# A four-layer graph network on one core: layer 3's tiles multiplied in runs of four, with a buffer pool shared with layer 2's edge tiles

## The chip, the cores and the metric

The kernel runs on one core of a Trainium2 chip. The core has five engines that matter here: TensorE (PE in the profile; PEld is its weight load), VectorE (DVE), ScalarE (ACT), GpSimd (POOL) and SyncE (SP). Each works through its own list of instructions in order, and they wait for each other by semaphores. The time is device microseconds from the runs of the whole program; the figure that counts is their median.

## The reference

There are 16 graphs of 1024 nodes with 256 features, and a symmetric 0/1 edge matrix for each. Four layers follow one another, each on a normalized input, with the input added to its result:

```python
h = jnp.maximum(_layernorm(x, axis=-1), 0.0)
x = x + _L0_gnn_ref(h, adj, L0_gnn_W, L0_gnn_a)       # attention, softmax over axis 1
h = jnp.maximum(_layernorm(x, axis=-1), 0.0)
x = x + _L1_gnn_ref(h, adj, L1_gnn_W, L1_gnn_a)       # attention, softmax over axis 2
h = jnp.maximum(_layernorm(x, axis=-1), 0.0)
x = x + _L2_gnn_ref(h, adj, L2_gnn_W_msg, L2_gnn_W_upd, L2_gnn_bias)
h = jnp.maximum(_layernorm(x, axis=-1), 0.0)
x = x + _L3_gnn_ref(h, adj, L3_gnn_W, L3_gnn_a_src, ...)
```

Layer 2 is the mean over the neighbours, a product of the edge matrix with the projected features:

```python
a = adj.astype(x.dtype)
h = jnp.einsum('bnf,fu->bnu', x, W_msg)
msg_sum = jnp.einsum('bij,biu->bju', a, h)
deg = jnp.sum(a, axis=1)
messages = jnp.where(deg[..., None] > 0, msg_sum / jnp.maximum(deg, 1.0)[..., None], 0.0)
out = jnp.einsum('bnf,fu->bnu', x, W_upd) + messages + bias
```

Layer 3 is an attention with four heads of 64 features, then a normalization over each head:

```python
weight = weight + mask * (e_src[:, :, t, :, None] + e_dst[:, :, t, None, :])
weight = jax.nn.leaky_relu(weight, negative_slope=0.01)
weight = jnp.where(node_adj[:, None] == 0, NEG, weight)
attention = jax.nn.softmax(weight, axis=-1)
dst = jnp.einsum('bhij,bhje->bhie', attention, h) + bias[None, :, None, :]
out = jax.nn.relu(dst) + h
```

## The kernel before

The kernel has two versions of the work; for these inputs the one in `tile_simple_stack` runs, and everything below is in it. A tile is 128 rows of a graph's 1024, so a graph has eight (NT).

**The order of the work.** Each graph is a Python generator that gives out its instructions and yields how many microseconds it thinks they take. The loop at the end takes the generators by their clocks: a graph starts 120 planned microseconds after the one before it (APART), and its own plan is about 260 long, so two graphs are always interleaved. By that plan layer 3 of a graph lies beside layer 0's products and layer 1's beginning of the next graph, and layer 2 beside layer 0's projections. The order of giving out is a priority, not the final order: when the program is built, the instructions of each engine are ordered by when they are estimated to be ready. `later` (`tc.keep_in_program_order`) pins an instruction behind the one given out before it on the same engine. A tile with a tag takes one of the tag's `bufs` buffers; the instruction that first writes it waits until a buffer has been released by the last user of its former tile.

**Layer 2** (`layer2`, from L890) multiplies the edge matrix as weights: for each of eight column blocks j, one edge tile of 512 KB (`load_adj`, L584, a DMA from GpSimd's queue at L589) is used by L922 with the projected features, split in a high and a low part. The tag "adj" has four buffers. Four tiles are loaded at the layer's start, and each block's end gives out the load four blocks on.

**Layer 3** (`layer3`, from L939): for each head h and each tile j, VectorE makes an attention tile p of 128x1024 by L968 from a row that lies in all partitions, a column q and the mask, in one instruction. TensorE then multiplies it (L981) as weights with the 64 features of the head and a column of sums, in halves of 64 columns, into two PSUM banks that hold all eight output tiles. The tiles are taken in runs of two; all products of a run follow its last p, since the first product of the run reads that one. The last graph takes runs of one. The tag "p3" has five buffers; two weight tiles at the start and `sq` in `tail` use it too.

Beside it on the engines are layer 0's products (L790), the transposes of the normalization (L684), the projections (L690), and layer 1's tiles p1 (L861) and products (L854). The rows of the attention layers go through DRAM: `spread` writes them (L709), `everywhere` reads them back into all partitions (L715), both from SyncE's queue, which also loads the pieces of the transposed edge matrix for the masks (raw, L568). ScalarE turns these into the mask bytes (L581). GpSimd makes the powers for the normalizations (`inv_std`, L596 and L597), and its queue issues the edge loads and the loads of x (L547).

Of the kernel before, what the change touches and what calls it, by code (L numbers as in the profile page):

```python
# [14 lines left out]
P = 128  # L15
# [406 lines left out]
def tile_simple_stack(  # L422
# [24 lines left out]
    HW = HO + 1  # L447
    STEP = 1.48
    EARLY = 2

    const = ctx.enter_context(tc.tile_pool(name="const", bufs=1))
    dram = ctx.enter_context(tc.tile_pool(name="dram", bufs=2, space=bass.MemoryType.DRAM))
# [44 lines left out]
    def weights01(layer, w, w_t, a, order, wait=True):  # L497

        wx[layer] = t = load_w(w, D, f"wx{layer}", D + 2, wait)
        wts = work.tile([P, N], F32, tag="p3", name="wts", bufs=5)[:, : DC * D].rearrange("p (c f) -> p c f", c=DC)  # L500
        if wait:
            behind(wts[:1, 0, :1])
        later(nc.sync.dma_start(wts, w_t.rearrange("(c p) f -> p c f", p=P)))
        avs = small.tile([P, DC, 2], F32, tag="avs", name="avs", bufs=1)
        later(nc.sync.dma_start(avs, a.rearrange("(c p) k -> p c k", p=P)))
        for fc in range(DC):
            ps = mm_ps.tile([P, HALF], F32, tag="mm", name="ps_wa")
            for ec in range(DC):
                nc.tensor.matmul(
                    ps[:, :2], wts[:, ec, fc * P : (fc + 1) * P], avs[:, ec, :], start=(ec == 0), stop=(ec == DC - 1)  # L510
                )
            for k, to in enumerate(order):
                nc.vector.tensor_copy(t[:, fc, D + to : D + to + 1], ps[:, k : k + 1])
# [11 lines left out]
    def weights3():  # L525

        wx[3] = t = load_w(w3, D, "wx3", W3)
        w3ts = work.tile([P, N], F32, tag="p3", name="w3ts", bufs=5)[:HO, :].rearrange("p (h f) -> p h f", h=H)
# [54 lines left out]

    def load_adj(b, g):  # L584

        t = state.tile([P, NT, EIGHTH], F32R, tag="adj", name="adj", bufs=4)
        if b == 0 and g < 4:
            behind(t[:1, 0, :1])
        nc.gpsimd.dma_start(t, adj[b, :, g * EIGHTH : (g + 1) * EIGHTH].rearrange("(i p) c -> p i c", p=P))  # L589
        return t  # L590


# [236 lines left out]
    def layer1(b, xs, mask, norm, after):  # L829
# [23 lines left out]
        def product(ps, i, j):  # L853
            nc.tensor.matmul(  # L854
                ps[:, : D + 1], ps_[j][:, i * P : (i + 1) * P], hs[:, j, : D + 1], start=(j == 0), stop=(j == NT - 1)
            )
# [9 lines left out]
        for i in range(NT):  # L866
            if i < len(early):
                ps = early[i]
            else:
                ps = at_ps.tile([P, HALF], F32, tag="at", name="ps_o1")  # L870
                for j in range(NT):
                    product(ps, i, j)
            k = b * NT + i
            z = shares[:, k : k + 1]
            nc.vector.reciprocal(z, ps[:, D : D + 1])
            e = work.tile([P, D], F32, tag="e", name="e")
            nc.scalar.activation(e, ps[:, :D], AF.Exp, scale=z)
# [13 lines left out]
    def layer2(b, xs, norm, after):  # L891
# [2 lines left out]

        adj_n = [load_adj(b, g) for g in range(4)]
        z = small.tile([P, NT], F32, tag="z2", name="z2", bufs=2)
        nc.vector.reciprocal(z, norm.times)
        hi = state.tile([P, NT, W3], F32R, tag="hs", name="hi", bufs=3)  # L900
# [12 lines left out]
        for j in range(NT):  # L913
# [10 lines left out]
                        start=False, stop=(h is lo and i == NT - 1), skip_group_check=True,  # L924
                    )
            k = b * NT + j
            if j + 4 < NE:
                adj_n.append(load_adj(b, j + 4))
            v = work.tile([P, D], F32, tag="v", name="v")
            nc.scalar.activation(v, ps[:, :D], AF.Copy, scale=z[:, j : j + 1])  # L930
            nc.scalar.copy(edges[:, k : k + 1], ps[:, D : D + 1])
# [5 lines left out]
    def layer3(b, xs, mask, norm, res):  # L937
        hs = new_hs()
        terms = hs[:, :, D:]  # L939
        run = 2 if b < B - 1 else 1  # L940
        hb = new_hs("hb")
        hbv = hb[:, :, : H * HW].rearrange("p t (h e) -> p t h e", e=HW)
        for n in range(NT):
# [17 lines left out]
        for h in range(H):  # L961
            next_row = everywhere(d_row[h + 1], "row3") if h + 1 < H else None
            pss = [hd_ps.tile([P, HALF], F32, tag="hd", name="ps_o3") for _ in range(NHALF)]
            for j in range(0, NT, run):
                ps_ = []
                for jj in range(j, j + run):
                    p = work.tile([P, N], F32, tag="p3", name="p3", bufs=5)
                    nc.vector.scalar_tensor_tensor(p, row, q[:, jj, h : h + 1], mask[:, jj, :], op0=OP.max, op1=OP.mult)  # L968
                    ps_.append(p)


                last = run - 1
                runs = [(last, 0), (last, PER)] + [(t, i) for t in range(run) for i in range(NT) if t < last or i % PER]
# [3 lines left out]
                for t, i in runs:  # L977
                    g, k = divmod(i, PER)
                    for c in range(2):
# [3 lines left out]
                            start=(j == 0 and t == last and k == 0), stop=(j == NT - run and t == last and k == PER - 1),  # L983
                            skip_group_check=True,
                        )
                yield 1.4 * run
            for g in range(NHALF):
                o = pss[g][:, : PER * HW].rearrange("p (k e) -> p k e", e=HW)
                nc.scalar.activation(res[:, g * PER : (g + 1) * PER, h, :], o, AF.Relu)  # L989
# [3 lines left out]
    def tail(b, xs, hs, res):  # L993
# [4 lines left out]
        for g in range(NHALF):  # L998
# [15 lines left out]
            sq = work.tile([P, N], F32, tag="p3", name="sq", bufs=5).rearrange("p (k e) -> p k e", e=HO)  # L1014
            nc.scalar.activation(sq, o, AF.Square)
            halves.append((t, o, of, m, sq))
        rs = []
# [45 lines left out]
        hs = yield from layer3(b, xs, m.bytes, norm, res)  # L1063
        return tail(b, xs, hs, res)

    loaded, masks = {}, {}

    def loads(b):
        loaded[b] = load_x(b)
# [109 lines left out]
```

## Time and profile before

| what | value |
|---|---|
| median of three runs | 2609.52 us (2608.33 to 2610.64) |
| the profiled execution: its time, its span | 2612.95 us, 2611.1 us |
| mean granted TensorE clock | 0.987 |
| instructions | 63088 |
| edge loads (L589): number, size, median from issue to landing | 128, 512 KB, 4.8 us |
| moved by DMA in all | 232.17 MB, 89 GB/s on average |

The span is what the hardware profiler saw from the first to the last instruction; the run's time has a little around it. In the pages a group of instructions has its line, its engine, what it writes and reads, how often it ran, its busy time, the mean of one, and the idle time of the engine just before it with what ended that. In a timeline each row starts with the start and the length in us, and the idle time before it stands in brackets. Of the waits, those of GpSimd are the longest (it waits for ScalarE 1537.6 us and for L922 477.9 us), but it is busy for only 17% of the span.

### The profile page before, as it was taken

How to read it: one execution, taken by the hardware profiler on the slowest of the kernel's cores; microseconds unless marked ns; L12 is line 12 of the kernel's file. 1: busy time of each engine (PE TensorE's matmuls, PEld its weight loads, DVE VectorE, ACT ScalarE, POOL GpSimd, SP SyncE). 2: the span in 40 equal slices, each digit the busy share in tenths (PEclk: the TensorE clock that was granted, in tenths of full speed). 3: DMA queues.
4: the chain of work that ended last, by engine and by line, in shares of the span. 5: the costliest groups of instructions: out<-in, count | busy, mean ns of one | idle time of the engine just before them, and what ended most of it. 6: DMA issues, size and time to landing. Idle time of an engine off the chain costs nothing.

```text
span 2611.1 us, 63088 instructions
## 1 busy us (share of the span) xinstructions
PE 2462.2 (94%) x26224; PEld 2102.5 (81%) x26224; DVE 1978.2 (76%) x3862; ACT 1431.3 (55%) x4036; POOL 449.9 (17%) x454
## 2 busy tenths in 40 slices
PE   6999999999999999999999999999999999999975
PEld 4788887888888888887888878888887888878864
DVE  6458778687777878778687777878768697777858
ACT  3763755637475563755637465563755637465350
POOL 1020211203021120211203021120211203011021
PEclk8999999999999999999999999999999999999987
DMA  4541522625225151522615224261522515224021
GB/s 136 111 85 55 141 54 78 130 66 131 62 89 103 62 134 55 134 58 80 132 59 137 63 86 105 63 134 55 134 58 80 133 57 138 64 67 103 25 65 36
DMA packets 212152, 232.17 MB, mean 89 GB/s; under 512 B 10344, under 2 KB 160976, under 8 KB 211856
## 3 DMA queue, kind: packets, MB, share of 16 engines
q1 hardware_dynamic: 74128, 144.14, 17.6%
q0 software_dynamic: 137728, 83.90, 17.2%
q8 instruction: 208, 3.41, 0.5%
q14 instruction: 88, 0.72, 0.1%
HBM read 210.78 MB, written 17.22 MB: 87 GB/s over the span
## 4 chain that ended last, share of the span: by engine, by line
PE 57%; DVE 17%; DMA 11%; ACT 10%; issue 3%; POOL 2%; SPq 0%; DVEq 0%; POOLq 0%; ACTq 0%
PE ps_o L790 16%; PE ps_proj L690 12%; PE ps_o L981 10%; DVE p L968 6%; PE ps_o L922 6%; PE ps_o L854 5%; DMA row<-d_row 5%; PE pt_h L684 5%; DVE p L861 4%; DMA raw<-in_adj_t 4%; PE ps_o L916 3%; ACT mask L581 2%; DMA d_row<-e_row 2%; ACT hn L671 2%; ACT unread L644 2%
## 5 line engine op out<-in xcount | busy, mean ns | idle before, releaser
L968 DVE SCALAR_TENSOR_TENSOR p<-row,q,mask 128x1024 f32<-128x1024 f32 x512 | 632.3, 1280 | 66.9 <-PE ps_o L981 55.7
L981 PEld LDWEIGHTS ps_o<-hb,p 128*64 128x64 f32 x16384 | 505.4, 138 | 101.8 <-DVE p L968 40.3
L981 PE MATMUL ps_o<-hb,p 128*64 128x65 f32 x16384 | 541.7, 224 | 28.7 <-DVE p L968 18.6
L690 PE MATMUL ps_proj<-wx,ht 128*128 128x258 f32 (+2 forms) x2048 | 509.8, 388 | 3.5 <-ACT hs L770 2.3
L790 PE MATMUL ps_o<-hs,p 128*128 128x256 f32 x2048 | 493.3, 386 | 18.8 <-ACT hs L804 18.8
L854 PE MATMUL ps_o<-hs,p 128*128 128x257 f32 x2048 | 496.9, 389 | 8.6 <-DVE p L861 8.6
L790 PEld LDWEIGHTS ps_o<-hs,p 128*128 128x128 f32 x2048 | 379.5, 191 | 75.0 <-ACT hs L804 23.2
L690 PEld LDWEIGHTS ps_proj<-wx,ht 128*128 128x128 f32 x2048 | 366.2, 191 | 77.2 <-ACT hs L770 9.7
L854 PEld LDWEIGHTS ps_o<-hs,p 128*128 128x128 f32 x2048 | 375.3, 191 | 62.9 <-DVE p L861 10.3
L596 POOL TENSOR_SCALAR rs<-mv 128x4 f32<-128x4 f32 (+1 forms) x112 | 41.2, 367 | 1557.4 <-ACT unread L644 1537.6
L597 POOL TENSOR_TENSOR rs<-rs,neg_half 128x4 f32<-128x4 f32 (+2 forms) x144 | 261.7, 1818 | 11.8
L759 DVE SCALAR_TENSOR_TENSOR xs<-e,xs 128x256 f32<-128x256 f32 x256 | 108.0, 422 | 180.7 <-ACT e L822 133.4
L671 ACT ACTIVATE hn<-xs,shift 128x256 f32<-128x256 f32 x384 | 175.2, 502 | 124.9 <-DVE shift L639 118.3
L684 PE MATMUL pt_h<-ident,hn 128*128 128x128 f32 x1024 | 181.8, 289 | 42.8 <-ACT hn L671 41.8
L922 PE MATMUL ps_o<-hi,adj 128*128 128x258 f32 x1024 | 203.2, 321 | 1.6
L684 PEld LDWEIGHTS pt_h<-ident,hn 128*128 128x128 f32 x1024 | 115.7, 142 | 110.0 <-ACT hn L671 93.2
L589 POOL DMA_DIRECT2D adj<-in_adj x128 | 114.5, 895 | 479.5 <-PE ps_o L922 477.9
L581 ACT ACTIVATE mask<-raw 128x512 uint8<-128x512 int32 x240 | 150.1, 626 | 69.7 <-DMA raw<-in_adj_t 42.8
L760 DVE SCALAR_TENSOR_TENSOR xs<-v,xs 128x256 f32<-128x256 f32 x384 | 161.4, 423 | 29.4 <-ACT v L824 16.5
L800 DVE SCALAR_TENSOR_TENSOR p<-row,q 128x1024 f32<-128x1024 f32 x128 | 161.8, 1274 | 18.5 <-DMA row<-d_row 16.9
L989 ACT ACTIVATE res<-ps_o 128x260 f32<-128x260 f32 x128 | 46.4, 374 | 232.4 <-PE ps_o L981 232.1
L922 PEld LDWEIGHTS ps_o<-hi,adj 128*128 128x128 f32 x1024 | 152.5, 190 | 14.2 <-ACT hi L908 4.8
(115 smaller groups left out, 3035.9 us busy)
## 6 DMA issues: line engine op xcount, KB each, us to landing
raw<-in_adj_t SPq DMA_DIRECT2D x256, 256.0 KB
adj<-in_adj POOLq DMA_DIRECT2D x128, 512.0 KB, 4.8
row<-d_row SPq DMA_DIRECT2D x109, 512.0 KB
xs<-in_x POOLq DMA_DIRECT2D x32, 512.0 KB, 7.1
out<-xs SPq DMA_DIRECT2D x32, 512.0 KB
wx<-in_w SPq DMA_DIRECT2D x3, 256.0 KB
d_row<-e_row SPq DMA_DIRECT2D x45, 4.0 KB
wts<-in_w_t SPq DMA_DIRECT2D x2, 256.0 KB
```

Source lines behind the costliest of these rows:

```text
L581: nc.scalar.activation(to, raw, AF.Square, accum_out=total)
L597: nc.gpsimd.tensor_tensor(rs[:, :n], rs[:, :n], neg_half[:, :n], op=OP.pow)
L671: nc.scalar.activation(hn, xs[:, 2 * g + k, :], AF.Relu, scale=scale, bias=bias)
L684: nc.tensor.transpose(pt[:, c, k * P : (k + 1) * P], hn[:, c * P : (c + 1) * P], ident)
L690: nc.tensor.matmul(ps[:, :width], norm.ht[:, c, n * P : (n + 1) * P], w[:, c, :width], start=(c == 0), stop=(c == DC - 1))
L760: nc.vector.scalar_tensor_tensor(x, v, 0.0, x, op0=OP.max, op1=OP.add, accum_out=after.sums[:, i % 2 : i % 2 + 1])
L790: m = nc.tensor.matmul(ps[:, :D], ps_[j][:, i * P : (i + 1) * P], hs[:, j, :D], start=(j == 0), stop=(j == NT - 1))
L800: nc.vector.scalar_tensor_tensor(p, row_a, q[:, j : j + 1], row_b, op0=OP.mult, op1=OP.max)
L854: nc.tensor.matmul(ps[:, : D + 1], ps_[j][:, i * P : (i + 1) * P], hs[:, j, : D + 1], start=(j == 0), stop=(j == NT - 1))
L922: nc.tensor.matmul(ps[:, : D + 2], adj_n[j][:, i, :], h[:, i, : D + 2], start=False, stop=(h is lo and i == NT - 1), skip_group_check=True,)
L968: nc.vector.scalar_tensor_tensor(p, row, q[:, jj, h : h + 1], mask[:, jj, :], op0=OP.max, op1=OP.mult)
L981: nc.tensor.matmul(pss[g][part, k * HW : (k + 1) * HW], ps_[t][:, i * P : (i + 1) * P][:, part], hbv[:, j + t, h, :], start=(j == 0 and t ...
```

## The change

Three things are changed together. Layer 3 takes its tiles in runs of four (the last graph still in runs of one), and inside a run it yields once in the middle, so that the planned pace per tile is as before. The tag "adj" is gone: the edge tiles take the tag "p3", which now has nine buffers, as many as the two tags had together, in the same size. And the edge loads are given out elsewhere: the first four of a graph in its layer 1, when the third output tile begins, the other four at the start of layer 2, all pinned with `later`.

```diff
+    P3 = 9
...
     def load_adj(b, g):
-        t = state.tile([P, NT, EIGHTH], F32R, tag="adj", name="adj", bufs=4)
+        t = work.tile([P, N], F32R, tag="p3", name="adj", bufs=P3).rearrange("p (i c) -> p i c", c=EIGHTH)
         if b == 0 and g < 4:
             behind(t[:1, 0, :1])
-        nc.gpsimd.dma_start(t, adj[b, :, g * EIGHTH : (g + 1) * EIGHTH].rearrange("(i p) c -> p i c", p=P))
+        later(nc.gpsimd.dma_start(t, adj[b, :, g * EIGHTH : (g + 1) * EIGHTH].rearrange("(i p) c -> p i c", p=P)))
         return t
...
                 for j in range(NT):
                     product(ps, i, j)
+            if i == 2:
+                first_adj[b] = [load_adj(b, g) for g in range(4)]
             k = b * NT + i
...
-        adj_n = [load_adj(b, g) for g in range(4)]
+        adj_n = first_adj.pop(b)
+        adj_n += [load_adj(b, g) for g in range(4, NE)]
...
             k = b * NT + j
-            if j + 4 < NE:
-                adj_n.append(load_adj(b, j + 4))
...
-        run = 2 if b < B - 1 else 1
+        run = 4 if b < B - 1 else 1
...
-                    p = work.tile([P, N], F32, tag="p3", name="p3", bufs=5)
+                    p = work.tile([P, N], F32, tag="p3", name="p3", bufs=P3)
                     nc.vector.scalar_tensor_tensor(p, row, q[:, jj, h : h + 1], mask[:, jj, :], op0=OP.max, op1=OP.mult)
                     ps_.append(p)
+                    if jj % 2 and jj + 1 < j + run:
+                        yield 2.8
...
-                yield 1.4 * run
+                yield 1.4 * min(run, 2)
```

The other users of "p3" (`wts`, `w3ts`, `sq`) get `bufs=P3` in place of 5, and `first_adj` is a new dictionary beside `loaded` and `masks`.

More of the change, by code (lines that the diff above doesn't have):

```diff
@@ L499, in weights01 @@
         wx[layer] = t = load_w(w, D, f"wx{layer}", D + 2, wait)
-        wts = work.tile([P, N], F32, tag="p3", name="wts", bufs=5)[:, : DC * D].rearrange("p (c f) -> p c f", c=DC)
+        wts = work.tile([P, N], F32, tag="p3", name="wts", bufs=P3)[:, : DC * D].rearrange("p (c f) -> p c f", c=DC)
         if wait:
@@ L527, in weights3 @@
         wx[3] = t = load_w(w3, D, "wx3", W3)
-        w3ts = work.tile([P, N], F32, tag="p3", name="w3ts", bufs=5)[:HO, :].rearrange("p (h f) -> p h f", h=H)
+        w3ts = work.tile([P, N], F32, tag="p3", name="w3ts", bufs=P3)[:HO, :].rearrange("p (h f) -> p h f", h=H)
         behind(w3ts[:1, 0, :1])
@@ L1013, in tail @@
             yield STEP
-            sq = work.tile([P, N], F32, tag="p3", name="sq", bufs=5).rearrange("p (k e) -> p k e", e=HO)
+            sq = work.tile([P, N], F32, tag="p3", name="sq", bufs=P3).rearrange("p (k e) -> p k e", e=HO)
             nc.scalar.activation(sq, o, AF.Square)
@@ L1064, in graph @@
         return tail(b, xs, hs, res)
-    loaded, masks = {}, {}
+    loaded, masks, first_adj = {}, {}, {}
     def loads(b):
```

## The prediction

> **What bounds the kernel now.** I began with the page: busy times first, then the costliest groups.
>
> ```profile
> PE 2462.2 (94%) x26224; PEld 2102.5 (81%) x26224; DVE 1978.2 (76%) x3862; ACT 1431.3 (55%) x4036; POOL 449.9 (17%) x454
> L968 DVE SCALAR_TENSOR_TENSOR p<-row,q,mask 128x1024 f32<-128x1024 f32 x512 | 632.3, 1280 | 66.9 <-PE ps_o L981 55.7
> L981 PEld LDWEIGHTS ps_o<-hb,p 128*64 128x64 f32 x16384 | 505.4, 138 | 101.8 <-DVE p L968 40.3
> L981 PE MATMUL ps_o<-hb,p 128*64 128x65 f32 x16384 | 541.7, 224 | 28.7 <-DVE p L968 18.6
> ```
>
> TensorE is the bound over the whole span. Only layer 3 shows the two waits the change is about: VectorE waits 55.7 us for TensorE to give p buffers back, TensorE 18.6 us for p. An average hides where, so next I took busy times in stretches of one layer 3, in the middle of the run (us from the span's start, then length, PE, PEld, DVE, ACT, POOL, clock, DMA). The same rows come back 157.0 us later, so it stands for the 15 graphs whose layer 3 lies beside the next graph's layers 0 and 1.
>
> ```profile
> 1303.00:1321.00 18.00, 18.00 (x345) 15.55 (x345) 17.07 (x21) 7.53 (x22) 2.20 (x2) 1.00 0.11 32
> 1321.00:1334.00 13.00, 12.72 (x247) 10.93 (x243) 8.45 (x9) 6.86 (x18) 0.00 (x0) 1.00 0.01 3
> 1334.00:1341.00 7.00, 5.43 (x165) 5.17 (x164) 5.74 (x6) 0.43 (x2) 0.00 (x0) 1.00 0.76 214
> 1341.00:1364.00 23.00, 21.96 (x392) 18.26 (x392) 22.92 (x41) 5.49 (x16) 0.00 (x0) 1.00 0.09 29
> ```
>
> TensorE bounds it up to 1334, VectorE from 1341 on (22.92 of 23 us), and between them both wait for a row. TensorE's idle time is 0 + 0.28 + 1.57 + 1.04 = 2.9 us a graph: nothing the change does to waits can bring more. Then the timeline of TensorE:
>
> ```profile
> 1313.36 3.95 PE L981 MATMUL ps_o<-hb,p 128*64 128x65 f32 x128
> ...
> 1324.40 2.09 PE L981 MATMUL ps_o<-hb,p 128*64 128x65 f32 x64
> 1326.42 2.88 PE L690 MATMUL ps_proj<-wx,ht 128*128 128x258 f32 x12
> 1329.23 2.09 PE L981 MATMUL ps_o<-hb,p 128*64 128x65 f32 x64
> ...
> 1340.71 1.13 PE L854 MATMUL ps_o<-hs,p 128*128 128x257 f32 x4 [1.57 <-DVE p L861]
> ...
> 1350.37 2.09 PE L981 MATMUL ps_o<-hb,p 128*64 128x65 f32 x64 [0.36 <-DVE p L968]
> ...
> 1355.06 2.09 PE L981 MATMUL ps_o<-hb,p 128*64 128x65 f32 x64 [0.68 <-DVE p L968]
> ```
>
> A run of two is 64 instructions, 32 for each p. Two in a row, 128, take 3.95 us: with 222 ns for the last, the pitch is 3.73/127 = 29.4 ns, so a p costs TensorE 0.94 us and VectorE 1.2 (six in 7.44 us). The timeline of VectorE shows where buffers lack, and that its order has a place for the row:
>
> ```profile
> 1321.01 2.48 DVE L968 SCALAR_TENSOR_TENSOR p<-row,q,mask 128x1024 f32<-128x1024 f32 x2 [0.79 <-PE ps_o L981]
> 1325.84 2.48 DVE L968 SCALAR_TENSOR_TENSOR p<-row,q,mask 128x1024 f32<-128x1024 f32 x2 [2.35 <-PE ps_o L981]
> ...
> 1330.67 7.44 DVE L968 SCALAR_TENSOR_TENSOR p<-row,q,mask 128x1024 f32<-128x1024 f32 x6 [0.57 <-PE ps_o L981]
> 1339.37 4.87 DVE L861 SCALAR_TENSOR_TENSOR p<-row,q,mask 128x1024 f32<-128x1024 f32 x4 [1.26 <-DMA row<-d_row]
> ```
>
> Last, GpSimd's timeline, for the edge loads (L589):
>
> ```profile
> 1259.85 0.88 POOL L589 DMA_DIRECT2D adj<-in_adj  x1 [1.89 <-PE ps_o L922]
> 1264.91 0.87 POOL L589 DMA_DIRECT2D adj<-in_adj  x1 [4.18 <-PE ps_o L922]
> ...
> 1317.97 1.93 POOL L597 TENSOR_TENSOR rs<-rs,neg_half 128x4 f32<-128x4 f32 x1
> 1376.19 0.45 POOL L596 TENSOR_SCALAR rs<-mv 128x4 f32<-128x4 f32 x1 [56.30 <-ACT unread L644]
> ```
>
> Eight loads start between 1251.7 and 1279.2, inside one layer 2. Four are its own second half; the last four, from 1264.91, are the next graph's first half, issued the moment a buffer comes free, over 100 us before their layer. So instructions are ordered by readiness, not by the place where they are given out.
>
> **What the Trainium skill says.** "TensorEngine Tiling (Array Packing)", Key Properties: changing the tiling mode drains TensorE. L981 uses half the columns (128*64), all else there 128*128. The trace agrees: from 1324.40 to 1329.23 are 4.83 us for 64 + 12 instructions; 64 x 0.0294 = 1.88, and twelve L690 at their own pitch, (2.88 - 0.39)/11 = 0.227, make 2.72; 0.23 us is left for one round trip. At L854's dense pitch of 0.218 (x72 in 15.88 us) it is 0.33. I take 0.3. "TensorE: Matmul & The Clock Gate", The mechanism: matmuls start and end in program order. So a run that waits for its p holds all behind it; the 1.57 us gap, with work queued behind, agrees. "DMA: Bandwidth & Descriptors", Issuing engines are not separate DMA queues: GpSimd's and SyncE's transfers share the same 16 engines. No isolated case in this trace proves it.
>
> **The change part by part.**
> *Runs of four.* 16 runs a graph become 8; no instruction is added or removed. Up to 1334 the trace has seven bursts of L981 with 676 instructions, 21 p; in fours that is some four, three round trips fewer: 3 x 0.3 = 0.9 us gained where TensorE is the bound. After 1341, seven bursts become three, but VectorE is the bound there and it brings nothing by itself. Bounds: 0 to 8 x 0.3 = 2.4.
>
> *Buffers.* Nine for p and edge tiles. The first four loads are pinned only behind GpSimd's instruction given out before them, the rs of layer 0's last tiles: 1317.97, done at 1319.9. GpSimd then has nothing until 1376. What they need besides is a free p3 buffer. Runs of four release one each 0.94 us while VectorE fills one each 1.2 us, so now and then a buffer is free with no p ready to take it; a load then holds it until the next layer 2, near 1408. I expect all four gone by about 1335, within two runs. Five are left, as before, but a run now needs four of them, not two.
> What that costs: in 1334 to 1341 TensorE has done 21.1 p of 23 made; in whole runs it can do 20, so 1.1 x 0.94 = 1.1 us more gap. Other side: VectorE gets ahead first and the gap of 1.57 goes. After 1341, a run waits for its fourth p. From 1345.3 to 1355.0 (p 25 to 28 made) TensorE has one run (3.8), sixteen L854 (3.5) and switches (0.6), 7.9 of 9.7 us: 1.8 idle for 1.04 now, 0.7 more. Other side: 1.0 less. Behind a p that waits on VectorE stand layer 1's p1 (L861) and the residuals, for which ScalarE waits, then the transposes.
>
> *Second half of the loads.* Four more are pinned behind the rs at 1392.42, done 1394.3, and find buffers at once. Four issues of 0.9 us hold GpSimd to 1398; the 15 us waits on L922, with xs loads (L547) behind, are gone and cost nothing today. But 2 MB now move from 1395, where before they came after 1408. raw alone runs at 187 GB/s there (8 x 256 KB in 11.35 us); at such a rate they last to 1406, and SyncE issues the two rows of layer 0 at 1402.4. Shared for 3 us, they lose between 0 and 3 us; VectorE already waits 0.82 us for them and TensorE 0.36 behind it, so nothing covers it. I take 0.7. The first half moves into 1320 to 1335, where DMA runs at 3 GB/s: nothing.
>
> *At no cost:* the shared tag for weights and sq (the tail needs two, five are free then), and the pacing, which keeps 5.6 for four p. The last graph runs by ones: VectorE feeds it at 1.2 us a p whatever the buffers.
>
> Sum: -0.9 + 1.1 + 0.7 + 0.7 = +1.6 us a graph, x 15 = +24. The profiled execution took 2612.95 us (span 2611.1), 3.4 above the median of the runs; on the median that is 2609.5 + 24 = 2633.
>
> **The rivals.**
> *Nine buffers stay with p (faster).* The loads find no free buffer until the last run is given its own. VectorE then fills the 4.55 us that it idles from 1321 to 1334 (13.00 - 8.45), nearly four p more; that covers the row gap and shortens the VectorE-bound part. Of 2.9 us idle 1.9 go, and four or five round trips, 1.3: -3.2 x 15 = -48, 2562. It decides as soon as two or more of the four loads start after the middle of layer 3. For it: buffer waits are real. Against: the early loads at 1264.91.
> *Loads late, on top of raw.* They start at 1355 to 1365, where eight raw loads feed ScalarE's masks in order and TensorE already idles 1.05 us at 1376.9. Doubling 2 MB can hold raw for up to 11 us, of which I take half, 5.5; less the 3.2: +2.3 x 15, 2644. For it: raw waits of 42.8 us on the page.
> *A draw.* Switches saved pay for the longer waits, TensorE being busy for all but 5 of 157 us: 2610.
>
> **How the numbers follow.** Forecast 0.42, late loads 0.20, draw 0.11, faster 0.27 (half of it at 2562 and half nearer to before). A measurement of this kernel tells about 0.2%, 5 us. Slower 0.62, same 0.11, faster 0.27. Adding the bounds: -2.4 - 1.6 - 1.0 = -5.0 to 1.1 + 1.5 + 3 = +5.6 us a graph, 2535 to 2694; all at one end is unlikely, so I cut to 2573 and 2672. The forecast's own range is 2615 to 2655.
>
> **What would show it.** Right: L589 starting in two groups, about 1320 to 1335 and after each layer 1; L981 in bursts of 128; PE's idle before L981 on L968 above 18.6 us; row waits at L800 above 16.9. Wrong: first loads after the last L968 of a graph; VectorE's 55.7 us on L981 nearly gone; shorter periods than 157.0.

## The result and the profile after

The changed kernel takes 2696.93 us (2691.95 to 2699.93, four runs) against 2608.93 us for the kernel before, run beside it: ratio 1.0334, 95% interval 1.0316 to 1.0352. It is slower by 88 us. The forecast was 2633 us, with a range of 2615 to 2655, so the direction was right and the size was not. The lines of the page after that answer to those shown before (p is now L970, its products are L984):

```profile
PE 2482.9 (92%) x26224; PEld 2106.0 (78%) x26224; DVE 1980.0 (73%) x3862; ACT 1437.0 (53%) x4036; POOL 432.2 (16%) x454
...
L970 DVE SCALAR_TENSOR_TENSOR p<-row,q,mask 128x1024 f32<-128x1024 f32 x512 | 630.5, 1278 | 47.3 <-PE ps_o L984 38.4
...
L984 PE MATMUL ps_o<-hb,p 128*64 128x65 f32 x16384 | 526.5, 224 | 29.3 <-DVE shares L878 12.8
...
L582 ACT ACTIVATE mask<-raw 128x512 uint8<-128x512 int32 x240 | 150.0, 625 | 130.5 <-DMA raw<-in_adj_t 102.6
...
L801 DVE SCALAR_TENSOR_TENSOR p<-row,q 128x1024 f32<-128x1024 f32 x128 | 161.1, 1269 | 31.7 <-DMA row<-d_row 30.1
```

The wait that the change is about has become shorter: VectorE waits 38.4 us for TensorE to release p tiles, where it waited 55.7. Two other waits have grown. ScalarE's mask instruction waits 102.6 us for its loads, where the page before has 42.8, and layer 0's p waits 30.1 us for its row, where it had 16.9. So time seems to have gone outside layer 3, and some of it to transfers; a wait on the page does not yet say what it cost.

To see where, I cut the period of a graph at two points that both traces have: the last p of layer 3, and the next p that layer 0 makes (it is for the graph after the next). The means are over the twelve graphs from the second to the thirteenth, worked out from the rows of L968/L970 and L800/L801. The middle stretch is cut once more, at the issue of the small write of layer 0's row (L709/L710) and of the read that follows it (L715/L716):

| us a graph | before | after | difference |
|---|---|---|---|
| layer 3: first p to last p | 57.27 | 55.58 | -1.69 |
| last p to layer 0's first p | 48.28 | 55.72 | +7.44 |
| ... of it: last p to the write | 40.00 | 44.43 | +4.43 |
| ... of it: the write to the read | 1.83 | 4.95 | +3.12 |
| ... of it: the read to layer 0's first p | 6.45 | 6.34 | -0.11 |
| layer 0's first p to layer 3's next first p | 51.58 | 51.54 | -0.04 |
| period | 157.14 | 162.85 | +5.71 |

In the middle stretch TensorE's idle time rises from 1.94 to 5.02 us. The whole is made up so: the first layer 3 begins at 214.2 us instead of 202.2, a single loss of 12.0, and from there to the last one the kernel loses 74.6 us more, which gives the 86.6 us by which the spans differ.

The middle stretch has two readings: one for the 3.12 us between write and read, one for the 4.43 us before it. The first is on GpSimd's and SyncE's timelines of the kernel after (start, length, issuing queue, transfer), around a graph whose last p ends at 1244.00:

```profile
1234.00 0.96 POOL L590 DMA_DIRECT2D adj<-in_adj  x1 [26.23 <-PE ps_o L984]
1239.91 1.80 POOL L590 DMA_DIRECT2D adj<-in_adj  x2 [4.95 <-DVE xs L760]
1242.11 0.87 POOL L590 DMA_DIRECT2D adj<-in_adj  x1 [0.40 <-issue]
...
1280.87 3.57 POOL L590 DMA_DIRECT2D adj<-in_adj  x4
```

```profile
1244.78 11.65 SPq L569 DMA_DIRECT2D raw<-in_adj_t  x8
...
1288.68 0.73 SPq L710 DMA_DIRECT2D d_row<-e_row  x2
1294.16 0.82 SPq L716 DMA_DIRECT2D row<-d_row  x2
```

The first four edge loads are issued in the last ten microseconds of layer 3, and the eight raw loads follow at once. The second four are issued together from 1280.87, just before SyncE writes the small attention row of layer 0 to DRAM (L710) and reads it back (L716). The chain of waits prices that meeting. Here it is in the kernel after, and then the same two pieces in the kernel before:

```profile
1288.68 5.46 DMA d_row<-e_row
...
1294.60 5.68 DMA row<-d_row
```

```profile
1243.76 1.75 DMA d_row<-e_row
...
1245.97 5.54 DMA row<-d_row
```

The write of 4 KB takes 5.46 us instead of 1.75 in these two graphs, while the read back is as long as it was. The graph shown is the longest of the twelve; in the mean the read follows the write 4.95 us later instead of 1.83. The trace's DMA packets, counted over the twelve graphs, show where the time goes: the first packet of the write starts 3.1 us after its issue instead of 1.0, and from there to the end of its last are 1.3 us instead of 0.45. Meanwhile some 1600 packets of GpSimd's edge loads start; in the kernel before there is none. Layer 0's p, and TensorE behind it, wait for both.

The second reading is TensorE's timeline near the same last p (1244.00), and that of the kernel before near its own (1203.44):

```profile
1238.22 3.95 PE L984 MATMUL ps_o<-hb,p 128*64 128x65 f32 x128 [0.86 <-DVE shares L878]
1242.10 2.00 PE L855 MATMUL ps_o<-hs,p 128*128 128x257 f32 x8
1244.05 3.95 PE L984 MATMUL ps_o<-hb,p 128*64 128x65 f32 x128
1247.94 5.47 PE L855 MATMUL ps_o<-hs,p 128*128 128x257 f32 x24
```

```profile
1197.56 2.09 PE L981 MATMUL ps_o<-hb,p 128*64 128x65 f32 x64 [0.68 <-DVE p L968]
1199.58 1.13 PE L854 MATMUL ps_o<-hs,p 128*128 128x257 f32 x4
1200.64 2.09 PE L981 MATMUL ps_o<-hb,p 128*64 128x65 f32 x64
1202.66 1.13 PE L854 MATMUL ps_o<-hs,p 128*128 128x257 f32 x4
1203.72 2.09 PE L981 MATMUL ps_o<-hb,p 128*64 128x65 f32 x64
```

A run of four cannot begin before its fourth p, so 3.95 us of products lie behind the last p, where 2.09 lay. Layer 3's products therefore end 4.0 us after the last p, instead of 2.4 (means of the twelve graphs, too): counted from the first p to the last product, layer 3 takes 59.6 us in the changed kernel and 59.7 in the kernel before. The 1.7 us by which the p tiles are earlier are not there at the end of the products. What stands behind them is later still. VectorE's timeline of the kernel after shows it:

```profile
1251.36 0.25 DVE L1007 RECIPROCAL m<-res 128x16 f32<-128x16 f32 x1 [1.34 <-ACT res L992]
1251.53 1.16 DVE L1012 TENSOR_REDUCE m<-res 128x16 f32<-128x1024 f32 x1
1252.61 0.15 DVE L878 RECIPROCAL shares<-ps_o 128x1 f32<-128x1 f32 x1
```

L878 is layer 1's next tile of the following graph. It comes 8.6 us after the last p (1252.61 - 1244.00); in the kernel before it came 5.1 us after (1208.58 - 1203.44); the means are 8.3 and 5.1. GpSimd begins the first power behind it (L598, before L597) 19.7 us after the last p instead of 15.8, and the write is issued 44.4 us after it instead of 40.0.

### The profile page after: what moved, and what is told of

Read it like the earlier page. It is cut to its first block, busy times and chain, and to the rows that moved or that the text cites. A ratio compares the mean times of both kernels' runs of the same rounds, so it can differ in the third digit from the quotient of the medians.

```text
span 2697.7 us, 63021 instructions
## 1 busy us (share of the span) xinstructions
PE 2482.9 (92%) x26224; PEld 2106.0 (78%) x26224; DVE 1980.0 (73%) x3862; ACT 1437.0 (53%) x4036; POOL 432.2 (16%) x454
## 4 chain that ended last, share of the span: by engine, by line
PE 39%; DVE 25%; DMA 15%; ACT 13%; issue 5%; POOL 3%; SPq 0%; DVEq 0%; ACTq 0%
PE ps_o L791 11%; DVE p L970 10%; PE ps_proj L691 9%; DMA raw<-in_adj_t 6%; PE ps_o L926 6%; DMA row<-d_row 5%; DVE p L862 5%; PE ps_o L984 5%; DMA d_row<-e_row 3%; PE pt_h L685 3%; ACT hn L672 3%; ACT unread L645 2%; PE ps_o L855 2%; PE ps_o L920 2%; ACT mask L582 2%
## 5 line engine op out<-in xcount | busy, mean ns | idle before, releaser
L970 DVE SCALAR_TENSOR_TENSOR p<-row,q,mask 128x1024 f32<-128x1024 f32 x512 | 630.5, 1278 | 47.3 <-PE ps_o L984 38.4
L984 PEld LDWEIGHTS ps_o<-hb,p 128*64 128x64 f32 x16384 | 501.0, 139 | 83.3 <-issue 38.6
L984 PE MATMUL ps_o<-hb,p 128*64 128x65 f32 x16384 | 526.5, 224 | 29.3 <-DVE shares L878 12.8
L597 POOL TENSOR_SCALAR rs<-mv 128x4 f32<-128x4 f32 (+1 forms) x112 | 35.3, 315 | 1446.2 <-ACT unread L645 1409.9
L598 POOL TENSOR_TENSOR rs<-rs,neg_half 128x4 f32<-128x4 f32 (+2 forms) x144 | 250.0, 1741 | 9.5
L685 PE MATMUL pt_h<-ident,hn 128*128 128x128 f32 x1024 | 188.0, 289 | 61.6 <-ACT hn L672 59.2
L926 PE MATMUL ps_o<-hi,adj 128*128 128x258 f32 x1024 | 217.8, 330 | 28.4 <-ACT hi L912 28.3
L582 ACT ACTIVATE mask<-raw 128x512 uint8<-128x512 int32 x240 | 150.0, 625 | 130.5 <-DMA raw<-in_adj_t 102.6
L801 DVE SCALAR_TENSOR_TENSOR p<-row,q 128x1024 f32<-128x1024 f32 x128 | 161.1, 1269 | 31.7 <-DMA row<-d_row 30.1
```

The source lines that it names most:

```text
L582: nc.scalar.activation(to, raw, AF.Square, accum_out=total)
L598: nc.gpsimd.tensor_tensor(rs[:, :n], rs[:, :n], neg_half[:, :n], op=OP.pow)
L685: nc.tensor.transpose(pt[:, c, k * P : (k + 1) * P], hn[:, c * P : (c + 1) * P], ident)
L801: nc.vector.scalar_tensor_tensor(p, row_a, q[:, j : j + 1], row_b, op0=OP.mult, op1=OP.max)
L926: nc.tensor.matmul(ps[:, : D + 2], adj_n[j][:, i, :], h[:, i, : D + 2], start=False, stop=(h is lo and i == NT - 1), skip_group_check=True,)
L984: nc.tensor.matmul(pss[g][part, k * HW : (k + 1) * HW], ps_[t][:, i * P : (i + 1) * P][:, part], hbv[:, j + t, h, :], start=(j == 0 and t ...
```

## The experiments

Two theories stood against each other at first: D, that the moved edge loads meet other transfers, and R, that the runs of four themselves cost time. The first expectations speak of 8.7 us lost and 2.8 us gained a graph; the means of the table above are 7.44 and 1.69. The kernels were run in four groups, each beside runs of the kernel before, whose median was 2611.5, 2613.21, 2606.63 and 2608.26 us in them; a ratio is to the median of its own group. Periods are those of one profiled execution each, over the same twelve graphs, which scatter by 0.65 to 1.4 us about their mean. TensorE's granted clock over these graphs was 1.000 in the kernel before, 0.997 in the kernel after and 0.990 to 1.000 in the experiments. A clock lower by 0.003 makes 0.5 us in 157, so a difference of that size between two periods is not read as the effect of an edit.

**Loads moved, runs left at two (e2).** In the changed kernel:

```diff
-        run = 4 if b < B - 1 else 1
+        run = 2 if b < B - 1 else 1
```

> The changed kernel with runs of two again: shared pool of nine and moved loads stay. Theory D (the moved edge loads collide with the transfers of the mask pieces, of layer 0's row and of its 4 KB write): the loss between the last L970 of a graph and the next layer 0's first p, 8.7 us a graph, stays and the 2.8 us gained inside layer 3 goes: about 2609 + 15 x 8.7 = 2740 us, at least 2690. Theory R (runs of four themselves: TensorE waits for the fourth p, and the late last run holds ScalarE): 2605 to 2625 us.

Measured: 2675.92 us, ratio 1.0244 (1.0227 to 1.0262), period 161.02. The time lies between the two theories' ranges: each is right in part. The loads and the common buffers alone make most of the loss, 3.88 us a graph; the runs of four add 1.83 on top (162.85 - 161.02). The last p is followed by the write after 41.2 us, against 44.4 with runs of four, and the write by the read after 5.2. This kernel shows one thing more: with nine buffers VectorE waits only 8.6 us for TensorE to release p tiles, where the kernel before has 55.7, and layer 3 still takes 57.14 us for 57.27. The waits for p buffers cost layer 3 next to nothing.

**The second four loads held back until the row has landed (e3).** They are given out during layer 2's projections, and the first of them waits for the next graph's layer 0 row by a copy of one element:

```diff
+        if g == 4 and b + 1 in row0:
+            nc.vector.tensor_copy(t[:1, 0, :1], row0[b + 1][:1, :1])
...
-        adj_n += [load_adj(b, g) for g in range(4, NE)]
...
+            if n == 2:
+                adj_n += [load_adj(b, g) for g in range(4, NE)]
```

> The changed kernel, with the second four loads of a graph held back until the next graph's layer-0 row is in place (a one-element copy from the row into the first of the four tiles). Theory D: the row is at its old time, some 5 of the 8.7 us come back: 2610 to 2635 us, and the write of d_row lands in about 2 us, not 5.5. Theory R: no change, 2690 to 2700 us.

Measured: 2644.89 us, ratio 1.0121 (1.0091 to 1.0150), period 158.94; some 10 us above the range of theory D, far below that of R. SyncE's timeline of this kernel has the two transfers next to each other again:

```profile
1265.61 0.64 SPq L712 DMA_DIRECT2D d_row<-e_row  x2
1266.85 0.82 SPq L718 DMA_DIRECT2D row<-d_row  x2
```

From the write to the read are 1.2 us, where the kernel after has 5.5 (1288.68 to 1294.16) and the kernel before 1.8; the means are 1.3, 4.95 and 1.8. Apart from a copy of one element nothing but the time of four loads was changed, and 3.91 us a graph came back. Write to read accounts for 3.67 of them. On the page the mask's wait for its loads falls from 102.6 to 53.3 us, but the write is issued as long after the last p as before (44.6 and 44.4 us), so these waits held up nothing that counts here. The other 1.80 us over the kernel before are untouched by it.

**The first four loads later as well (e4)**, with `if i == 4` in place of `if i == 2`.

> As the run before, and the first four loads are given out at the fifth output tile of layer 1, not the third, so behind the powers of its first half, when the mask pieces have been read. Theory D: all 8.7 us come back and the 2.8 us stay: about 2565 to 2600 us, faster than the kernel before. Theory R: 2690 to 2700 us.

Measured: 2656.29 us, ratio 1.0180 (1.0157 to 1.0202), period 160.39: the expectation failed, it is worse than without it. GpSimd issued the four loads from 1240.04 to 1243.6, between two of its own powers, and the second of the powers behind layer 1 came 23.7 us after the last p instead of 20.9 (means). An issue that costs GpSimd 0.9 us is only free where GpSimd has nothing to do; that these issues, and not the loads' traffic, cost the time is argued from the timeline and was not tested apart.

**Four of the eight loads left out (e5).** Layer 2 takes the first four tiles twice.

> The changed kernel without the second four edge loads of each graph (layer 2 uses the first four tiles twice, so its sums are others). Theory D: as with the second half held back, 2605 to 2635 us, since 2 MB a graph no longer meet the row. Theory R: 2690 to 2700 us.

Measured: 12301.67 us, a time that says nothing of the loads, since the edge sums that layer 2 makes along the way are then others than the mask's and the program runs its general version after this one. The trace of the first part can be read: its period is 158.84, against 158.94 with the loads held back. Second loads that are held back are as good as none.

**The last run of four made two runs of two (e6).** On top of the held-back loads, in the last head alone:

```diff
+            sizes = [run] * (NT // run)
+            if h == H - 1 and run == 4:
+                sizes[-1:] = [2, 2]
```

> e3_gate_second with one more edit: the last head's last four tiles are multiplied in two runs of two, all other runs stay at four. Theory that the late last run delays layer 1 (its products end about 4.0 us after the last p, against 2.4 before, and everything behind them on ScalarE and GpSimd comes 3.6 to 3.8 us later): the stretch from the last p to layer 0's next p falls from 52.2 to 49 to 50.5 us, while layer 3's own stretch stays near 55.6 to 56.3; period 156 to 157.3, time 2600 to 2622 us. Rival, that the runs of four do no harm and the rest of e3's loss is still the transfers: no change, period 158.6 to 159.2, time 2638 to 2650 us.

Measured: 2660.95 us, ratio 1.0192 (1.0161 to 1.0222), period 159.99. The expectation failed: it did not become faster. How much slower it became is less sure than the numbers look, since the granted clock over the twelve graphs was 0.992, where the kernel it is built on had 1.000; on 153 us of TensorE's work a graph that makes 1.2 us, and the period grew by 1.05. TensorE's and VectorE's timelines near the last p (1227.97) show why nothing was gained:

```profile
1217.60 3.73 PE L858 MATMUL ps_o<-hs,p 128*128 128x257 f32 x16
1222.19 7.93 PE L992 MATMUL ps_o<-hb,p 128*64 128x65 f32 x256 [0.86 <-DVE shares L881]
1230.05 11.00 PE L858 MATMUL ps_o<-hs,p 128*128 128x257 f32 x48
```

```profile
1234.64 1.21 DVE L1021 TENSOR_REDUCE m<-res 128x16 f32<-128x1024 f32 x1
1235.78 0.15 DVE L881 RECIPROCAL shares<-ps_o 128x1 f32<-128x1 f32 x1
```

The last run did end earlier, 2.1 us after the last p. But all 256 instructions of the last head stand in one piece, and no product of layer 1 stands between them. Layer 1's next tile begins after the piece with all its 16 instructions, and its reciprocal comes 7.8 us after the last p, behind the tail's reductions. This speaks against the length of the last run and for the place of layer 1's products in the order.

**Runs of two with the held-back loads (e7).** The second experiment with the runs of the first:

> e3_gate_second with runs of two throughout, so the nine shared buffers and the moved, gated loads without the runs of four. Theory that the runs of four cost time of their own: 10 to 25 us below e3 (2620 to 2635 us), period 157.6 to 158.2, of which 0.5 to 1.1 us is the first half of the loads meeting the mask's loads. Rival, that the runs of four save their 1.7 us a graph and only the loads cost: 2655 to 2675 us, above e3.

Measured: 2623.35 us, ratio 1.0038 (1.0024 to 1.0053), period 157.63. With both known causes out, 0.49 us a graph over the kernel before is left, of which the granted clock (0.998) can make 0.3. Runs of four cost 1.31 here (158.94 - 157.63), and the time agrees with that theory.

**The split with the first graph's loads later (e8)**, by `if i == (4 if b == 0 else 2)`.

> e6_split_last with one more edit: in the first graph alone the first four edge loads are given out after the fifth node tile of layer 1 and not after the third. If the later first p of layer 3 (214 us against 202) is these four 512 KB loads standing in front of the first graph's other work, the first p comes back to 201 to 205 us and the time falls by 8 to 12 us below e6's; if the start-up delay has another cause, the two times agree within 3 us.

Measured: 2651.26 us, ratio 1.0142 (1.0109 to 1.0176), with the first p at 209.2 us instead of 211.3. The median fell by 9.7 us, but the profiled spans, 2655.7 and 2658.2, differ by 2.5 and the first p did not come back. The median is as the first expectation has it, the first p as the second has it. This decides nothing.

**Runs of four alone (e1).** In the kernel before, with the loads where they were, but with six p tiles and only three edge tiles, which is what fits:

> The kernel before with the runs of four alone: the edge loads stay in layer 2, in three buffers of their own and not four, and the p tiles get six and not five, which is what fits. Theory that the late last run costs: period 157.9 to 158.8, time 2620 to 2640 us, the stretch after the last p longer by 2.5 to 4 us and layer 3's shorter by 1 to 1.7. Theory that only the transfers cost: 2585 to 2611 us. If three edge buffers starve layer 2, its matmuls show waits on the adj transfer, and that is to be taken off first.

Measured: 2656.80 us, ratio 1.0167 (1.0135 to 1.0199), period 160.40. That is more than either theory had. VectorE's p tiles wait 75.4 us for TensorE, more than in any other kernel here: a run of four holds four of six buffers until its last p is made. Layer 3 gains nothing at all (57.35 us, against 55.6 with nine buffers). Layer 2 hardly suffers from its three buffers: its products wait 4.4 us for edge tiles in the whole run. The stretch behind the last p is 3.14 us longer than before (51.42), as the first theory had it, and here the edge loads are still in layer 2: write to read takes 1.3 us. So the runs of four lengthen that stretch by themselves; what they cost in all this kernel does not tell, since with six buffers they gain nothing in return.

**The last head in runs of two, three heads in runs of four (e9),** with the held-back loads:

```diff
+            run = 1 if b == B - 1 else 4 if h < H - 1 else 2
```

> e3_gate_second with the last of layer 3's four heads multiplied in runs of two, the other three heads in runs of four. e6 split the last run alone and TensorE still did the last head's 256 products in one piece, with no product of layer 1 between them. Theory that this missing interleaving is what delays layer 1 (its next node tile has all 16 products behind the piece, where before had half of them in front): the stretch from the last p to layer 0's first p falls from 52.2 to 49.2 to 49.8 us, layer 3's own stretch is 55.8 to 56.4, period 156.3 to 157.2, time 2605 to 2620 us. Rival, that any run of four delays what follows: 2635 to 2660 us.

Measured: 2618.05 us, ratio 1.0045 (1.0028 to 1.0061), period 156.97. Time and period are as the first theory has them. Layer 3 is at 55.45 us, and the stretch behind it at 50.29 is a little above what was expected. TensorE's timeline of this kernel, whose last p ends at 1207.42:

```profile
1202.92 3.95 PE L988 MATMUL ps_o<-hb,p 128*64 128x65 f32 x128
1206.81 0.70 PE L858 MATMUL ps_o<-hs,p 128*128 128x257 f32 x2
1207.48 2.09 PE L988 MATMUL ps_o<-hb,p 128*64 128x65 f32 x64
1209.49 10.23 PE L858 MATMUL ps_o<-hs,p 128*128 128x257 f32 x46
```

One run of 64 stands behind the last p again, and two instructions of layer 1's next tile in front of it; the reciprocal comes 6.3 us after the last p. By the periods, all runs of four together cost 1.31 us a graph; with the last head in twos they gain 0.66 (156.97 against 157.63), so the last head alone costs 1.97. The times say less: the profiled execution of this kernel was the fastest of its six (2611.37 us). The ratios 1.0121 and 1.0045 put the cost of the last head at some 20 us, 1.3 a graph, and 1.0045 against the 1.0038 of runs of two throughout shows no gain from the other three heads.

**Loads given out in their old place, from nine common buffers (e10, e11, e12).** Three kernels: runs of four, the same without the last head, and runs of four in the last head only.

> The kernel after with the edge loads given out where the kernel before gives them out (four ahead of layer 2, one more after each of its tiles), in the nine shared buffers: the runs of four alone. Theory that the runs of four cost by the order on TensorE and the loads by meeting other transfers, each by itself: the difference of e3 and e7 again, +1.0 to +1.5 us a graph, layer 3 at 55.5 to 55.8 us and the stretch behind it at 51 to 51.6, time 2625 to 2640 us. Rival, that without the moved loads the runs of four gain: 2585 to 2608 us. A time of 2650 us or more would say that the six p tiles and three edge buffers of e1 were not what cost there.

> e10 with the last head in runs of two. If the runs of four cost only through the last head's missing interleaving, what they save in the other three heads is left: layer 3 at 55.8 to 56.4 us, the stretch behind it at 48.3 to 48.9 as before, period 156.0 to 156.8, time 2592 to 2607 us, faster than before. Rival, that they save nothing at the end of the products: 2607 to 2618 us.

> The reverse of e11: runs of two in the first three heads, runs of four in the last head alone, loads as in the kernel before. Theory of the missing interleaving: the stretch behind the last p 2.5 to 3.2 us longer than before's 48.3, layer 3 at 56.6 to 57.2, period 159 to 160.2, time 2640 to 2660 us, the slowest of the three. Rival, that the cost is spread over all runs of four: 2610 to 2622 us.

Measured: 2675.70 us (ratio 1.0268, 1.0245 to 1.0291), 2659.97 us (1.0201, 1.0178 to 1.0224) and 2694.35 us (1.0339, 1.0315 to 1.0363), periods 161.37, 161.07 and 163.12. All three missed by far, by 30 us and more. GpSimd's timeline of the second (last p at 1229.10):

```profile
1252.38 1.85 POOL L590 DMA_DIRECT2D adj<-in_adj  x2
1254.30 0.93 POOL L597 TENSOR_SCALAR rs<-m 128x16 f32<-128x16 f32 x1
1255.29 0.92 POOL L590 DMA_DIRECT2D adj<-in_adj  x1
1256.23 4.01 POOL L598 TENSOR_TENSOR rs<-rs,neg_half 128x16 f32<-128x16 f32 x1
1260.20 4.43 POOL L590 DMA_DIRECT2D adj<-in_adj  x5
```

The text of the loads is in its old place, but their order is not. In the kernel before, each load waited for one of four buffers that an earlier block of layer 2 released, and that wait spread them over the layer. With nine buffers free, all eight go out at once, between GpSimd's powers and ahead of the row of layer 0. These three kernels therefore measure a third placing of the loads, as bad as the change's own, and do not answer what they were made for. What this placing costs lies elsewhere: in the second of the kernels write to read takes only 2.4 us in the mean, but the write is issued 45.5 us after the last p, where the kernel before has 40.0. Within the three the last head in fours is again the slower choice: by the medians all heads in fours take 15.7 us more than three heads, 1.0 a graph, and the last head alone in fours takes 34.4 more than the other three, 2.3 a graph. The periods have 0.30 and 2.05; the granted clock was 0.995, 0.990 and 0.994, lowest in the kernel that the other two are compared with, so both are too small.

**The third head in runs of two as well (e13),** on top of the kernel with the last head in twos.

> e9_last_head_twos with the third head in runs of two as well, so that only heads one and two have runs of four; loads gated as there. e9's stretch behind the last p is 50.3 us, 1.1 longer than with runs of two throughout (e7, 49.2). Theory that a run of four costs layer 1 wherever layer 1's products should stand between the runs, that is in heads three and four, where layer 1 of the next graph lies beside layer 3: the stretch comes to 49.0 to 49.5 us, layer 3 at 55.8 to 56.4, period 156.2 to 156.8, and the time is level with or below before, 2598 to 2612 us. Rival, that the 1.1 us has another source: the stretch stays at 50 to 50.6, layer 3 loses part of what it gained, 2618 to 2628 us.

Measured: 2618.05 us, ratio 1.0046 (1.0032 to 1.0060), period 156.89, layer 3 at 55.51 and the stretch behind it at 50.18. So it is the rival in the stretch, while layer 3 kept what it had gained: the third head's runs are worth nothing that can be seen either way, and the 1.1 us by which this stretch is longer than with runs of two (49.18) has another source. It is there by layer 1's next tile: its reciprocal comes 6.3 us after the last p, where it comes 5.1 us after with runs of two. The period is 0.25 us shorter than that of the kernel before, too little to be read from one profile each, and the first layer 3 begins at 213.0 us instead of 202.2. The time is above that of the kernel before, and no version here beats it.

**The changed kernel with the last head alone in runs of two (e14),** its loads as the change has them.

> The changed kernel with one thing undone: the last of layer 3's four heads in runs of two; its loads stay where the change put them, ungated. If the order on TensorE in the last head costs in the changed kernel what it cost in the gated one (e3 less e9, 1.97 us a graph): period 160.6 to 161.2, time 2660 to 2675 us. If the 5.5 us that the small write waits for the second half of the loads hides it: 2685 to 2700 us.

Measured: 2670.19 us, ratio 1.0250 (1.0236 to 1.0264), period 160.96, as the first theory has it. One line of the loop is worth 1.89 us a graph in the changed kernel too, at the same granted clock (0.997); the ratios 1.0334 and 1.0250 put it at some 22 us, 1.5 a graph. SyncE's timeline shows that the other cause is still there in full:

```profile
1273.22 0.68 SPq L710 DMA_DIRECT2D d_row<-e_row  x2
1278.69 0.82 SPq L716 DMA_DIRECT2D row<-d_row  x2
```

From the write to the read are 5.5 us, as in the kernel after. The second cause does not hide the first: undoing the last head's runs is worth about the same with the loads' meeting and without.

## Why the prediction was wrong

The prediction's sum was +1.6 us a graph, and +5.71 was measured. The 2697 us lie beyond even the sum of its upper bounds, 2694. Two kernels that lie between before and after split the loss into three steps:

| step | period, us | cost a graph | ratio to before |
|---|---|---|---|
| before | 157.14 | | 1 |
| nine common buffers, first four loads moved, second four held back (runs of two) | 157.63 | +0.49 | 1.0038 |
| second four loads as the change has them | 161.02 | +3.39 | 1.0244 |
| runs of four | 162.85 | +1.83 | 1.0334 |

The prediction had -0.9 for switches, +1.1 and +0.7 for waits in layer 3, and +0.7 for the second four loads. The largest part of what it missed, 2.7 of 4.1 us, is the last of these terms. The other steps that failed are the buffers and the end of the last run.

*Second half of the loads: the mechanism was right, the term mis-sized.* The collision was predicted, with the four loads at the start of layer 2, in GpSimd's idle time, and moving while the row is on its way. It was priced at 0.7 us, with 3 as the upper bound, and measured 3.39 (3.91 with runs of four). The sum looked at the wrong transfer. It let the two row reads of 512 KB share bandwidth with the loads, and those are as long as before (5.68 and 5.54). What is hurt is the 4 KB write in front of them, which the prediction did not price: with runs of two, write to read takes 5.19 us in the mean with these loads and 1.41 without, which covers the whole step. "DMA: Bandwidth & Descriptors" in the Trainium skill, section Issuing engines are not separate DMA queues, was quoted beside the statement that no isolated case proves it. Holding the loads back is that case: transfers issued by GpSimd hold up a write of another queue. The section gives no figure for it; here it is 3.1 to 3.8 us in the mean. What the write waits for before its first packet is not separated. The last raw load stands in front of it on SyncE's queue and is late as well: in the graph shown its packets begin 4.1 us after its issue, where in the kernel before they begin after 1.0. So the write can wait for the engines or for that load.

*Buffers: the mechanism failed.* "I expect all four gone by about 1335, within two runs" did not happen. In the kernel after GpSimd waits 26.23 us for TensorE to release the first buffer, and the loads start in the last ten microseconds before the last p. So no p lacked a buffer on account of a load, and the +1.1 and +0.7 were for a case that did not occur; TensorE's idle time in layer 3 rose by 0.8 us, from 2.36 to 3.17. The +0.9 that these terms and the switches make together has the right sign by luck. The stretch that they were read from was not typical either: 157 us after the 1334 to 1341 of the prediction TensorE is busy for 6.70 us of the same 7 and not 5.43, so the rows do not all come back, and the 2.9 us of idle time are 2.36 in the mean. That a buffer stays with p for as long as p tiles are asked for was the rival "nine buffers stay with p", and VectorE's shorter wait bears it out, 38.4 us with runs of four and 8.6 with runs of two. But the rival's gain did not come: with runs of two, layer 3 is as long as before; with runs of four it is shorter up to the last p only. The place of the loads was that of the rival "loads late, on top of raw". They do meet the raw loads, but it had priced 5.5 us for that. The step that contains this meeting, with the new buffers, costs 0.49.

*Runs of four: a term was missing.* The prediction saved switches and asked what a run waits for, but did not ask what lies behind the last run of a graph. What it missed is the last head: 1.89 us in the changed kernel and 1.97 in the one with the loads held back, or 1.5 and 1.3 by the times. There layer 1 of the next graph is the work that sets the end, and its products lose their place between the runs. That the length of the last run is the cause was my next theory, and it fell with the split. That it is the last head is shown by two kernels that undo its runs of four and get the time back. That it is the order there is argued from the timelines, which show what comes late: from the first p of layer 3 to the reciprocal of layer 1's next tile are 62.3 us with runs of two, 64.1 with runs of four and 61.7 with the last head in twos (loads held back in all three), and these differences, +1.8 and -0.6, go with those of the periods, +1.31 and -0.66. No kernel moved layer 1's products alone.

*Switches: not settled.* With the last head in twos and the loads held back, the runs of four gain 0.66 us a graph by the periods, where 0.9 was estimated. Up to half of this can be the clock (0.998 against 1.000), the ratios show no gain, and what part the switches have in it was not isolated.

*Open:* the later beginning of the first layer 3, 12.0 us in the profile. It varies from 204.1 to 209.7 us over the three kernels with the loads in their old place, whose text up to layer 3's runs is the same, so it is not the text alone. Most of it goes with TensorE's granted clock, the third figure from the end of these rows for the time up to the first p, first in the kernel before, then after:

```profile
0.00:202.20 202.20, 172.27 (x833) 142.58 (x834) 111.26 (x353) 111.96 (x305) 30.37 (x42) 0.94 0.47 112
```

```profile
0.00:214.20 214.20, 178.62 (x834) 147.24 (x835) 112.04 (x355) 112.15 (x305) 27.33 (x38) 0.90 0.38 96
```

Clock that was not granted makes 11.9 us in the first and 20.5 in the second (from the unrounded shares), 8.6 of the 12.0 between them. Over all sixteen kernels here the first p comes at 202.2 to 214.2 us; less the clock that was lost it comes at 190.3 to 194.7. Why less clock was granted, and whether an edit has a part in it, is not shown. The 1.1 us behind the last p that remain with only two heads in fours are open too.

## What to carry to other kernels

Before a load is moved to an idle stretch, look for the small transfers in it: a 4 KB write on the critical path lost 3.1 us in the mean to four large loads, more than half of the whole loss a graph. A pool's size can be what spaces loads out; when buffers are added or shared, ask what now starts all at once. And when work is put in larger pieces, look at the end of the stage, at what stood between the small pieces and is now behind the large one; larger pieces in the early heads gained 0.66 us a graph at best, and in the last head they cost 1.3 to 2. Last, compare the granted clock of two profiles before a difference of half a microsecond is read as an effect.

## What was not expected of the hardware

A write of 4 KB took 1.75 us without and 5.46 us with four 512 KB loads of another engine under way, while the 512 KB row reads behind it were not slowed by more than 0.14 us (5.54 and 5.68). Two thirds of the delay passed before its first packet had started (3.1 us in the mean instead of 1.0). The median edge load took 6.9 us to land instead of 4.8. GpSimd was busy 0.90 us for each of these loads' issues (the mean of 128), and where four of them stood between two of its powers, the second power came 2.8 us later.
